# Five channels per selection matmul in the last group of a convolve-and-whiten kernel, and one load of the last pass moved

## The chip, the cores and the metric

The kernel runs on one core of a Trainium2 chip. The metric is the device time of one execution in microseconds (us). Engines are named as the profile names them: PE is TensorE (PEld its weight loads), DVE is VectorE, ACT is ScalarE, POOL is GpSimd, and SP is SyncE, which here issues most DMAs.

## The reference

The input x has 4 images of 64 channels of 256 x 256 pixels, f32. Layer 0 convolves every channel with its own 256 x 256 filter, which is the outer product of two filters of length 256 (each made by a small sine network), and adds `x * bias`. Layer 1 whitens the channels: the covariance of every ninth pixel, five Newton-Schulz steps towards its inverse square root, and that 64 x 64 matrix applied to all pixels.

```python
k = einsum('ijk,imk->ijmk', hx, hy)[0]            # separable filter of each channel
y = irfft2(rfft2(x, 512) * rfft2(k, 512) / 512)[..., :256, :256]
x = y + x * bias[:, None, None]
# layer 1
x1 = transpose(x, (1, 0, 2, 3)).reshape(64, -1)
x1_s = x1[:, ::9]                                  # every ninth pixel
mean1 = mean(x1_s, axis=-1, keepdims=True)
cov = x1_s @ x1_s.T / x1_s.shape[1] + 0.01 * eye(64)
out = newton_schulz_isqrt(cov, 5) @ (x1 - mean1)
```

## The kernel before

**First pass.** The work is cut into 32 steps `(g, n)`: a group g of 8 channels (`CG`) of image n. Step i holds its pixels in a buffer of `xpool`, which has four, so step i uses buffer i % 4. A step is done two channels at a time (c = 0, 2, 4, 6). `group` (L394) does the row convolution of two channels and the column convolution of the two channels of two positions earlier, as Toeplitz matmuls on PE. ACT copies the first result back, DVE adds `x * bias` to the second one in place (L412). Then `store` (L420) issues the two DMAs that write these channels to `y_d` in device memory, and `pack(2.92)` (L385) takes some operations from the list `todo`. The last two positions of the last step, (31, 4) and (31, 6), have no partner and go through `half_group(item, 1)` (L266), whose additions on DVE are those of L289; `pack(1.0)` follows each.

**Sampling.** Layer 1 needs every ninth pixel, and 256 is no multiple of 9, so each row of an image has its own phase. `pack_ops` (L313) gathers the samples of some channels into `samp[n]` with nine `copy_predicated` on DVE, one for each phase (L319); its source is every ninth element of a row. In the last two groups of channels a step hands over its first four channels as soon as they are stored, and its last four two positions later. `todo` takes the operations in order, each with a cost, and `pack` runs as many as its credit allows. The last four channels of the very last step, (7, 3), are packed by PE: `pack_by_pe` (L294) multiplies every ninth column of the pixels with `pick[:, s]`, a 128 x 128 selection matrix of phase s, and sums nine products in PSUM. It works on two channels at a time, for both halves b of the image's rows in one PSUM tile, and copies the result into `samp[3]` (L309, L311).

**Covariance and whitening.** `covariance(n)` (L327) multiplies the samples of an image, 58 matmuls (L333). After that of the last image a serial chain of small operations on PE, DVE and ACT (`whitening`, L460) makes the matrix W. `spin` (L437) issues matmuls whose result nobody reads. A matmul of f32 operands shows as two records of a weight load and two of a matmul in the profile.

**Last pass.** The 64 channels are read back from `y_d` in 32 pieces of 2 MB (`load_y`, L352), multiplied with W (L635), shifted by ACT and DVE (L639, L640) and stored (L645). Thirteen pieces have a home before any is stored: `homes` (L347) lists the pool of each, reusing buffers that the first pass has let go. The loads of pieces 0 to 8 are issued inside the first pass, at the places listed in `early` (L378), each behind the group of that place; pieces 9 to 12 come after the last matmuls of the first pass (L613). Piece 6 takes the buffer of step 29. Later loads wait until an earlier piece is stored.

**Order.** All instructions of the five engines of the first pass stand in the order in which the program writes them (`manual_schedule`); SP issues its DMAs in that order too.

The end of the first pass reads:

```python
for item in pending:              # (31, 4) and (31, 6)
    half_group(item, 1)
    pack(1.0)
    store(item)
pack()
...
for lo in range(CG // 2, CG, 2):
    pack_by_pe(g, n, yt, slice(lo, lo + 2))
spin(4)
covariance(NB - 1)
while len(loaded) < len(homes):
    load_next()
W, shift = whitening(i15, ones)
```

Of the kernel before, what the change touches and what calls it, by code (L numbers as in the profile page):

```python
# [38 lines left out]
F32 = mybir.dt.float32  # L39
# [7 lines left out]
P, H2 = 128, 2  # L47
EMB, ORDER = 33, 64
PIX = L * L
CG = 8  # L50
HP = P // 2
STEP = 9
NJ = 29
# [11 lines left out]
def conv_whiten_kernel(ctx: ExitStack, tc: tile.TileContext, a: dict, out: bass.AP):  # L65
    nc = tc.nc
# [9 lines left out]
    psA = ctx.enter_context(tc.tile_pool(name="psA", bufs=8, space=bass.MemoryType.PSUM))  # L76
# [23 lines left out]
    def load_x(t, g, n, c):  # L100
        nc.sync.dma_start(
            out=t[:, c : c + 2],
            in_=x[n, g][:, c : c + 2],
        )


    steps = [(g, n) for g in range(C // CG - 2) for n in range(NB)]
# [12 lines left out]
    samp = []  # L120
# [12 lines left out]
    def load_pick(lo, hi):  # L133
        for s in range(lo, hi):
            nc.scalar.activation(pick[:, s, :], ident, AF.Copy, scale=rows[:, s : s + 1])
# [47 lines left out]
    def new_toeplitz(g):  # L183


        return tpool.tile([P, 2, CG, L], F32, tag="toep", name=f"toep_{g}")

    def load_toeplitz(t, g, f, half, lo=0, hi=CG, issue=nc.sync):
        source, row = (g0_d, f * CG + lo) if g == 0 else (g_d, f * C + g * CG + lo)


        skip = 0 if f == half else HP
        issue.dma_start(
            out=t[half * HP : (half + 1) * HP, f, lo:hi, skip:],
            in_=bass.AP(
                tensor=source.tensor,
                offset=source.offset + row * GW + skip,
                ap=[[1, HP], [GW, hi - lo], [1, L - skip]],
            ),
        )  # L200
# [90 lines left out]
                        ALU.mult, ALU.add,  # L291
                    )

    def pack_by_pe(g, n, yt, cs):  # L294

        pk = psA.tile([P, H2, cs.stop - cs.start, NJ], F32, tag="psA", name=f"pk_{cs.start}")
        for s in range(STEP):
            for b in range(H2):
                nj = (L - s + STEP - 1) // STEP
                nc.tensor.matmul(  # L300
                    pk[:, b, :, 0:nj],
                    lhsT=pick[:, (s - b) % STEP, :],
                    rhs=yt[:, cs, b, s : s + STEP * (nj - 1) + 1 : STEP],
                    start=(s == 0 and b == 0),
                    stop=(s == STEP - 1 and b == H2 - 1),
                    skip_group_check=True,
                )
        dst = samp[n][:, :, :, g * CG + cs.start : g * CG + cs.stop]
        nc.scalar.copy(dst[:, 0], pk[:, 0].rearrange("p c j -> p j c"))  # L309
        copy = nc.vector.tensor_copy if cs.stop == CG else nc.scalar.copy  # L310
        copy(dst[:, 1], pk[:, 1].rearrange("p c j -> p j c"))  # L311

    def pack_ops(g, n, yt, cs):  # L313
        def op(s):
            nj = (L - s + STEP - 1) // STEP
            src = yt[:, cs, :, s : s + STEP * (nj - 1) + 1 : STEP].rearrange("p c b j -> p b j c")
            dst = samp[n][:, :, 0:nj, g * CG + cs.start : g * CG + cs.stop]
            m = mask[:, n, :, s : s + 1].unsqueeze(3).to_broadcast([P, H2, nj, cs.stop - cs.start])
            nc.vector.copy_predicated(dst, m, src)  # L319

        cost = 0.3 + 1.5e-3 * H2 * NJ * (cs.stop - cs.start)
        return [(cost, lambda s=s: op(s)) for s in range(STEP)]
# [4 lines left out]
    def covariance(n):  # L327

        pc = psA.tile([P, C + 1], F32, tag="psA", name=f"pc{n}")
        for b in range(H2):  # L330
            for j in range(NJ):
                half = slice(C * (j % 2), C * (j % 2 + 1))
                nc.tensor.matmul(  # L333
                    pc[half],
                    lhsT=samp[n][:, b, j, 0:C],
                    rhs=samp[n][:, b, j, :],
                    start=(b == 0 and j < 2),
                    stop=(b == H2 - 1 and j >= NJ - 2),
                    skip_group_check=True,
                )  # L340
        nc.vector.scalar_tensor_tensor(cov, pc, 1.0 / NSAMP, cov, ALU.mult, ALU.add)
# [18 lines left out]
    def load_next():  # L360
        loaded[len(loaded)] = load_y(len(loaded))

    loaded = {}
    todo = []
# [7 lines left out]
    for g in range(1, C // CG):  # L372
# [3 lines left out]
            blocks[k // 4, k % 4 * 2] = (g, part)  # L376

    early = {  # L378
        (26, 4): 1, (27, 0): 1, (27, 4): 1, (28, 0): 1, (29, 2): 1, (30, 0): 1, (31, 0): 1, (31, 2): 1, (31, 4): 1
    }  # L380
    orders = [list(range(L // HP)), list(reversed(range(L // HP)))]

# [2 lines left out]
    def pack(time=math.inf):  # L385
        credit[0] += time
        while todo and credit[0] > 0:
            cost, op = todo.pop(0)
            op()
            credit[0] -= cost  # L390
        if not todo:
            credit[0] = min(credit[0], 0.0)
# [27 lines left out]
    def store(second):  # L420
        g, n, c, yt, _ = second
        halves = g >= C // CG - 2
        for b in range(H2):
            row = b * C + g * CG + c
            nc.sync.dma_start(
                out=y_d[n][row : row + 2, :].rearrange("c (p w) -> p c w", w=L),
                in_=yt[:, c : c + 2, b],
            )

        if c == CG - 2 and (g, n) != steps[-1]:  # L430
            todo.extend(pack_ops(g, n, yt, slice(CG // 2 if halves else 0, CG)))
        elif c == CG // 2 - 2 and halves:
            todo.extend(pack_ops(g, n, yt, slice(0, CG // 2)))

    spins = []

    def spin(times):  # L437

        p = psA.tile([P, P], F32, tag="psA", name=f"spin{len(spins)}")
        spins.append(p)  # L440
        for _ in range(times):
            nc.tensor.matmul(p, lhsT=ident, rhs=ident, start=True, stop=True)  # L442
# [114 lines left out]
    with tc.manual_schedule(  # L557
        engines={engines.PE, engines.SP, engines.DVE, engines.Activation, engines.Pool}
    ):
        toep = {0: new_toeplitz(0)}  # L560

        for f, lo, hi in ((0, 0, 2), (0, 2, 4), (0, 4, 6), (1, 0, 2), (0, 6, 8), (1, 2, 4), (1, 4, 8)):
            for half in range(2):
                load_toeplitz(toep[0], 0, f, half, lo, hi, nc.scalar if half else nc.sync)
        for c in range(0, CG, 2):
            load_x(x_tiles[1], *steps[1], c)
        for i, (g, n) in enumerate(steps):
            xt = x_tiles[i % 4]
            for c in range(0, CG, 2):
                item = (g, n, c, xt, [])  # L570
                if g == C // CG - 1 and n > 0 and c == 2:
                    covariance(n - 1)
                if len(pending) == 2:
                    group(item, pending.pop(0))
                else:
                    half_group(item, 0)
                pending.append(item)
                if i == 0 and c == 6:

                    fold = const.tile([P, C], F32, tag="fold", name="fold")  # L580
                    nc.vector.tensor_tensor(fold, ident[:, 0:C], ident[:, C:P], ALU.add)

                    nc.scalar.activation(bf[:, 0:1], samp[0][:, 0, 0, C : C + 1], AF.Sqrt)
                if i == 1 and c < CG - 2:
                    load_pick(c // 2 * 3, c // 2 * 3 + 3)

                if i + 2 < len(steps):
                    load_x(x_tiles[(i + 2) % 4], *steps[i + 2], c)
                if (i, c) in blocks:
                    tg, part = blocks[i, c]  # L590
                    if part == 0:
                        toep[tg] = new_toeplitz(tg)
                    lo = part % 2 * CG // 2
                    load_toeplitz(toep[tg], tg, part // 4, part // 2 % 2, lo, lo + CG // 2)
                for _ in range(early.get((i, c), 0)):
                    load_next()
        g, n, c, yt, _ = pending[0]
        for item in pending:
# [5 lines that stand above are left out]
        i15 = place(2 * C, rows=C).rearrange("p (u c) -> p u c", u=2)  # L604
        for u in range(2):
            nc.gpsimd.tensor_scalar(i15[:, u], ident[0:C, 0:C], 1.5, None, ALU.mult)  # L606
        ones = place(P, rows=C)
        nc.gpsimd.memset(ones, 1.0)
        for lo in range(CG // 2, CG, 2):
            pack_by_pe(g, n, yt, slice(lo, lo + 2))  # L610
        spin(4)
        covariance(NB - 1)
        while len(loaded) < len(homes):  # L613
            load_next()
        W, shift = whitening(i15, ones)
# [3 lines left out]
    for i, (n, q) in enumerate(pieces):  # L619
        yt = loaded.pop(i)  # L620
# [5 lines left out]
        for w in range(FP // 1024):  # L626
# [6 lines left out]
            for k in range(2):  # L633
                for u in range(2):
                    nc.tensor.matmul(  # L635
                        po[u][halves[k]], lhsT=W[halves[u]], rhs=v[halves[u], k, cols],
                        start=True, stop=True,
# [68 lines left out]
```

## Time and profile before

| | |
|---|---|
| time, median of 3 runs | 903.08 us (902.95 to 903.26) |
| profiled execution | 903.93 us, of which the span from first to last instruction is 902.1 us |
| PE busy | 781.2 us, 87% of the span |
| DVE busy | 581.5 us, 64% |
| ACT busy | 395.5 us, 44% |
| DMA | 285.61 MB moved, 317 GB/s over the span |
| first pass: last Toeplitz matmul ends | about 619.4 us |
| covariance of the last image begins | 628.45 us |
| first matmul of the last pass | 643.18 us |

The profile is of one execution. A line of the timeline gives the start in us from the span's beginning, the duration, the engine, the source line, the operation, the tiles that it writes and reads, how many instructions were merged into the line, and in brackets the idle time before it and what ended it. A view by windows gives for stretches of time how long each engine was busy and, as the last two numbers, the mean busy share of the 16 DMA engines and the rate that they moved; such a share can come out a little above 1.

### The profile page before, as it was taken

The numbers are of one execution on the slowest core, as the hardware profiler recorded it, in microseconds if no ns is written. First come the engines' busy times: TensorE is split into PE (matmuls) and PEld (weight loads), VectorE is DVE, ScalarE is ACT, GpSimd is POOL, SyncE is SP. The second block draws the span as 40 slices with busy tenths as digits, with TensorE's granted clock in tenths as the row PEclk, the third lists the DMA queues.
The fourth block names the chain that finished last, engine by engine and source line by source line (L and its number), as shares of the span: only waits on it lengthen the run. The fifth ranks groups of instructions, "written<-read, shape, count | busy, mean of one in ns | idle before, by whom it ended". The sixth has DMA issues, their size and how long they took to land.

```text
span 902.1 us, 28046 instructions
## 1 busy us (share of the span) xinstructions
PE 781.2 (87%) x11928; PEld 647.5 (72%) x11928; DVE 581.5 (64%) x801; ACT 395.5 (44%) x676; POOL 14.5 (2%) x40
## 2 busy tenths in 40 slices
PE   8999999999999999999999999999999565666200
PEld 7999999999999999999999999999533111212000
DVE  3487778877888778877888877877688332233200
ACT  2655554545455555545454444442487232233200
POOL 1000000000000000000000000000010000000000
PEclk9999999999999999999999999999999766866755
DMA  7988889798788888888997899979999999999998
GB/s 209 327 262 252 242 261 271 234 273 251 247 263 261 244 264 259 258 250 267 293 275 241 285 351 356 335 237 390 375 401 429 430 432 432 429 434 430 430 430 355
DMA packets 117912, 285.61 MB, mean 317 GB/s; under 512 B 8891, under 2 KB 91116, under 8 KB 110108
## 3 DMA queue, kind: packets, MB, share of 16 engines
q1 hardware_dynamic: 113436, 244.94, 79.0%
q0 software_dynamic: 3056, 37.95, 10.0%
q8 instruction: 95, 1.56, 0.7%
q10 hardware_dynamic: 1296, 0.93, 0.4%
q14 instruction: 29, 0.24, 0.1%
HBM read 149.35 MB, written 134.44 MB: 315 GB/s over the span
## 4 chain that ended last, share of the span: by engine, by line
PE 74%; DMA 11%; another core or an unknown queue 7%; DVE 0%; issue 0%; SPq 0%; ACT 0%; POOLq 0%; DVEq 0%
PE p L220 64%; DMA out_dram<-yi 5%; DMA yi<-y_d 5%; PE po L635 4%; PE pc L333 2%; PE ph L252 1%; PE pk L300 1%; PE spin L442 1%; DMA toep<-g_d 0%; PE busy L152 0%; PE pm L158 0%; SPq L357 0%; DMA scratch<-in_zw_dram 0%; DVE yi L640 0%
## 5 line engine op out<-in xcount | busy, mean ns | idle before, releaser
L220 PE MATMUL p<-toep,x 64*64 64x64 f32 (+3 forms) x5040 | 579.5, 284 | 0.8 <-issue 0.8
L220 PE MATMUL p<-toep,o 64*64 64x64 f32 (+3 forms) x5040 | 579.5, 284 | 0.0
L220 PEld LDWEIGHTS p<-toep,x 64*128 64x128 f32 (+1 forms) x5040 | 535.7, 166 | 24.4 <-issue 1.3
L220 PEld LDWEIGHTS p<-toep,o 64*128 64x128 f32 (+1 forms) x5040 | 536.7, 166 | 10.7 <-issue 0.2
L409 ACT COPY o<-p 64x512 f32<-64x512 f32 x504 | 292.8, 581 | 294.2 <-PE p L220 286.6
L319 DVE COPY_PREDICATED samp<-mask,x 128x464 f32<-128x464 int32 (+3 forms) x351 | 297.2, 847 | 9.8 <-DVE x L412 0.2
L412 DVE SCALAR_TENSOR_TENSOR x<-x,bias,p 128x512 f32<-128x512 f32 x252 | 179.8, 744 | 121.3 <-PE p L220 117.3
L635 PE MATMUL po<-yi,chain 64*64 64x512 f32 x1024 | 143.7, 720 | 60.4 <-DMA yi<-y_d 60.4
L640 DVE TENSOR_SCALAR yi<-po,shift 128x512 f32<-128x512 f32 x128 | 96.1, 751 | 109.0 <-PE po L635 100.7
L635 PEld LDWEIGHTS po<-yi,chain 64*64 64x64 f32 x1024 | 48.0, 162 | 155.2 <-issue 150.5
L639 ACT ACTIVATE yi<-po,shift 128x512 f32<-128x512 f32 x128 | 88.0, 687 | 116.7 <-PE po L635 116.0
L333 PE MATMUL pc<-samp 128*64 128x65 f32 x464 | 14.9, 223 | 0.0
L333 PEld LDWEIGHTS pc<-samp 128*64 128x64 f32 x464 | 14.3, 137 | 0.3
L645 POOL DMA_DIRECT2D out_dram<-yi x19 | 10.5, 554 | 130.5 <-DMA out_dram<-yi 55.1
L606 POOL TENSOR_SCALAR chain<-ident 64x64 f32<-64x64 f32 x2 | 1.0, 519 | 606.6 <-PE ph L252 606.6
L286 DVE COPY o<-ph 64x256 f32<-64x256 f32 x8 | 3.4, 422 | 9.7 <-PE ph L252 9.6
L152 PE MATMUL busy<-idle 128*128 128x128 f32 x64 | 9.4, 307 | 0.0
L152 PEld LDWEIGHTS busy<-idle 128*128 128x128 f32 x64 | 8.9, 222 | 0.2 <-issue 0.2
L300 PE MATMUL pk<-x,pick 128*128 128x56 f32 (+1 forms) x72 | 8.3, 292 | 0.0
L300 PEld LDWEIGHTS pk<-x,pick 128*128 128x128 f32 x72 | 8.1, 192 | 0.1
L442 PE MATMUL spin<-ident 128*128 128x128 f32 x50 | 7.9, 292 | 0.0
L286 ACT COPY o<-ph 64x256 f32<-64x256 f32 x8 | 2.9, 368 | 10.7 <-DMA toep<-g_d 9.2
(93 smaller groups left out, 77.4 us busy)
## 6 DMA issues: line engine op xcount, KB each, us to landing
x<-in_x_dram SPq DMA_DIRECT2D x128, 512.0 KB, 5.3
y_d<-x SPq DMA_DIRECT2D x256, 256.0 KB, 3.5
yi<-y_d SPq DMA_DIRECT2D x32, 2048.0 KB, 15.6
out_dram<-yi POOLq DMA_DIRECT2D x17, 2048.0 KB, 67.7
out_dram<-yi SPq DMA_DIRECT2D x11, 2048.0 KB, 32.9
toep<-g_d SPq DMA_DIRECT2D x28, 256.0 KB, 6.3
toep<-g_d SPq DMA_DIRECT2D x29, 192.0 KB, 5.7
out_dram<-yi SPq DMA_DIRECT2D x4, 1024.0 KB, 32.8
```

The costliest lines, as they stand in the source:

```text
L152: nc.tensor.matmul(p, lhsT=idle[:, 0:P], rhs=idle[:, P : 2 * P], start=True, stop=True)
L220: mm = nc.tensor.matmul(ps[q : q + w, m, HP * k : L], lhsT=src[parts, k // 2, m * P + q : m * P + q + w], rhs=t[parts, : stop : -1] if k e ...
L300: nc.tensor.matmul(pk[:, b, :, 0:nj], lhsT=pick[:, (s - b) % STEP, :], rhs=yt[:, cs, b, s : s + STEP * (nj - 1) + 1 : STEP], start=(s == 0 ...
L319: nc.vector.copy_predicated(dst, m, src)
L333: nc.tensor.matmul(pc[half], lhsT=samp[n][:, b, j, 0:C], rhs=samp[n][:, b, j, :], start=(b == 0 and j < 2), stop=(b == H2 - 1 and j >= NJ ...
L409: nc.scalar.copy(o1[to], units[u][0][0][fr])
L412: nc.vector.scalar_tensor_tensor(x2[:, c2 + u], x2[:, c2 + u], bias[:, ch : ch + 1], units[u][1][0], ALU.mult, ALU.add,)
L442: nc.tensor.matmul(p, lhsT=ident, rhs=ident, start=True, stop=True)
L635: nc.tensor.matmul(po[u][halves[k]], lhsT=W[halves[u]], rhs=v[halves[u], k, cols], start=True, stop=True,)
L639: nc.scalar.activation(v[:, 0, cols], po[0], AF.Identity, bias=shift)
L640: nc.vector.tensor_scalar(v[:, 1, cols], po[1], shift, None, ALU.add)
L645: issue.dma_start(out=o[:, :, end - part : end], in_=v[:, :, end - part : end])
```

## The change

Three things change.

- Of the last step's eight channels DVE packs the first three instead of four (`LATE = 3`), so its nine `copy_predicated` there work on three channels each.
- `pack_by_pe` packs the other five in one go. There is one PSUM tile for each half b, and each selection matmul has five channels as its moving operand, 145 or 140 columns, where there were 58 or 56. So there are 18 matmuls where there were 36, and two copies of 145 elements a partition where there were four of 58: the first by ACT, the second by DVE. Five `spin` matmuls are put ahead of them.
- In `early` the load of piece 6 moves from (31, 0) to (30, 6), the position before it. SP issues it behind the group of that position, ahead of the two stores of (31, 0) that it followed before.

```diff
-    def pack_by_pe(g, n, yt, cs):
-        pk = psA.tile([P, H2, cs.stop - cs.start, NJ], F32, tag="psA", name=f"pk_{cs.start}")
-        for s in range(STEP):
-            for b in range(H2):
+    LATE = 3
+    def pack_by_pe(g, n, yt):
+        cs = slice(LATE, CG)
+        for b in range(H2):
+            pk = psA.tile([P, CG - LATE, NJ], F32, tag="psA", name=f"pk_{b}")
+            for s in range(STEP):
                 nj = (L - s + STEP - 1) // STEP
                 nc.tensor.matmul(
-                    pk[:, b, :, 0:nj],
+                    pk[:, :, 0:nj],
                     lhsT=pick[:, (s - b) % STEP, :],
                     rhs=yt[:, cs, b, s : s + STEP * (nj - 1) + 1 : STEP],
-                    start=(s == 0 and b == 0),
-                    stop=(s == STEP - 1 and b == H2 - 1),
+                    start=(s == 0),
+                    stop=(s == STEP - 1),
                     skip_group_check=True,
                 )
-        dst = samp[n][:, :, :, g * CG + cs.start : g * CG + cs.stop]
-        nc.scalar.copy(dst[:, 0], pk[:, 0].rearrange("p c j -> p j c"))
-        copy = nc.vector.tensor_copy if cs.stop == CG else nc.scalar.copy
-        copy(dst[:, 1], pk[:, 1].rearrange("p c j -> p j c"))
+            copy = nc.vector.tensor_copy if b else nc.scalar.copy
+            copy(samp[n][:, b, :, g * CG + LATE : (g + 1) * CG], pk.rearrange("p c j -> p j c"))
...
     early = {
-        (26, 4): 1, (27, 0): 1, (27, 4): 1, (28, 0): 1, (29, 2): 1, (30, 0): 1, (31, 0): 1, (31, 2): 1, (31, 4): 1
+        (26, 4): 1, (27, 0): 1, (27, 4): 1, (28, 0): 1, (29, 2): 1, (30, 0): 1, (30, 6): 1, (31, 2): 1, (31, 4): 1
     }
...
         elif c == CG // 2 - 2 and halves:
-            todo.extend(pack_ops(g, n, yt, slice(0, CG // 2)))
+            todo.extend(pack_ops(g, n, yt, slice(0, LATE if (g, n) == steps[-1] else CG // 2)))
...
-        for lo in range(CG // 2, CG, 2):
-            pack_by_pe(g, n, yt, slice(lo, lo + 2))
+        spin(5)
+        pack_by_pe(g, n, yt)
         spin(4)
         covariance(NB - 1)
```

## The prediction

> **What bounds the kernel.** I read the slices first (PE 0.9 busy up to 620 us, DMA at about 430 GB/s from 700 us on, so two stages with different limits), then the windows around the turn, with the DMA's share and rate as the last two numbers.
>
> ```profile
> 590.00:600.00 10.00, 10.00 (x235) 9.41 (x234) 8.88 (x16) 4.65 (x8) 0.00 (x0) 1.00 0.39 128
> 600.00:606.00 6.00, 6.00 (x88) 5.60 (x82) 2.81 (x6) 2.23 (x4) 0.00 (x0) 1.00 1.05 380
> 606.00:608.00 2.00, 2.00 (x32) 1.98 (x31) 1.65 (x3) 0.10 (x1) 0.00 (x0) 1.00 0.60 202
> 608.00:644.00 36.00, 34.83 (x460) 31.50 (x460) 22.16 (x59) 7.29 (x22) 1.15 (x3) 1.00 1.02 402
> 644.00:647.00 3.00, 3.00 (x32) 1.07 (x28) 2.31 (x4) 2.17 (x4) 0.00 (x0) 1.00 0.38 155
> 647.00:700.00 53.00, 52.67 (x493) 18.67 (x489) 45.86 (x62) 41.97 (x62) 6.79 (x12) 1.00 1.01 411
> 700.00:880.00 180.00, 87.17 (x504) 27.95 (x496) 47.97 (x64) 43.85 (x64) 3.74 (x7) 0.69 1.01 430
> ```
>
> From 608 us to the end the DMA is full, except at 644 to 647, where 0.62 x 3 = 1.86 us are lost: the 13 pieces that have a home have landed, and the first store is issued only at 645.57. After it, the remaining stores and loads run at the DMA's rate. So whatever delays the first store lengthens the kernel one for one; whatever hastens it gains at most these 1.86 us, about 0.2% (1.8 us), which is also about what a measurement of this kernel can tell from no change. What the first store waits for is the serial chain from the last Toeplitz matmul. The timeline of its PE part, then DVE's:
>
> ```profile
> 619.32 8.28 PE L300 MATMUL pk<-x,pick 128*128 128x58 f32 x72
> 627.42 1.10 PE L442 MATMUL spin<-ident 128*128 128x128 f32 x8
> 628.45 3.71 PE L333 MATMUL pc<-samp 128*64 128x65 f32 x116
> ```
> ```profile
> 618.59 1.30 DVE L319 COPY_PREDICATED samp<-mask,x 128x232 f32<-128x232 int32 x2
> 619.78 1.64 DVE L289 SCALAR_TENSOR_TENSOR x<-x,bias,ph 128x256 f32<-128x256 f32 x4
> 621.34 4.55 DVE L319 COPY_PREDICATED samp<-mask,x 128x232 f32<-128x232 int32 x7
> 627.89 0.22 DVE L311 COPY samp<-pk 128x58 f32<-128x58 f32 x1 [1.99 <-ACT samp L309]
> ```
>
> PE packs channels 4 and 5 while DVE's L289 still finishes 6 and 7 (to 621.42). The covariance (L333) starts 1.03 us after the spins do; the copies, done at 628.11, are hidden beneath them. Everything from L333 to the first store (645.57) is unchanged, so the question is when L333 starts.
>
> **When the new packing starts.** It needs channels 3 to 7, so the last L289. `copy_predicated` takes 627 ns for 232 elements and 1008 ns for 464 (the groups by form), 1.64 ns an element; three channels have 58 elements fewer, 0.095 us. Two of the nine lie ahead of that L289 (the order of the two kernels has the same two there): 621.42 - 0.19 = 621.23, and 0.06 us for the hand-over (L470 ends 633.06, its matmul's weights start 633.12): **621.3**, against 619.32. The five spins (10 records of 0.112 us, 1.1 us) fit into 619.4 to 621.3, where PE would wait: no cost. The other seven DVE operations end 0.85 us sooner, near 625.05, and matter only if PE is done by then.
>
> **What one record costs.** The 72 records of L300 come every 0.112 us (8.04 us from the first weight load to the first spin's), whether 58 or 56 columns: the load of 128 weight columns sets this pace, since the spins, with 128 columns, keep it too. With 16 records of 145 columns and 20 of 140 the moving operand takes over, and it is read with a step of nine elements. No such row is streaming bound, so I bound it:
>
> - *Below*: contiguous operands. 64x256 matmuls of L220 follow each other on one row tile every 0.214 us, 0.83 ns a column: 16 x 0.121 + 20 x 0.117 = **4.3 us** for the 36.
> - *Lag*: record by record, a matmul starts behind its own weight load by the streaming time of the matmul before: 54 ns after 64 contiguous columns, 107 to 110 after 128. In L300 it is 67 to 68 ns after 58 columns and 63 to 64 after 56, where contiguous ones would give 48 and 47. As a rate that is 1.15 ns a column: **5.9 us**.
> - *First of a group*: it starts with its weight load, so its duration shows its streaming.
>
> ```profile
> L300 PE MATMUL pk<-x,pick x72: 287/291/351, 619.3 to 627.3; 128*128 128x56 f32 x40, 128*128 128x58 f32 x32
> L457 PE MATMUL pw<-chain,chain x2: 272/296/321, 642.2 to 642.3; 64*128 64x65 f32 x2
> L442 PE MATMUL spin<-ident x50: 275/275/377, 627.4 to 643.0; 128*128 128x128 f32 x50
> ```
>
>   The maxima (third number) are these: 321 ns for 65 contiguous columns, 377 for 128, 0.89 ns a column; 351 for 58 strided ones is as many as 99 contiguous, 1.7 times the rate, 1.42 ns a column: **7.3 us**.
> - *Above*: two columns more lengthen the lag by 4 ns, 2 ns a column, as if a buffer hid a fixed part of a slower reading; 58 columns within 0.112 us cap it at 1.93 ns: **9.9 us**.
>
> I take twice the contiguous rate, 1.67 ns a column, between the last two: 16 x 0.242 + 20 x 0.233 = **8.5 us**. Twice the rate with 18 columns read ahead gives lags of (58 - 18) x 1.67 = 67 ns and (56 - 18) x 1.67 = 63 ns, both as read; a constant extra of 19 ns a record would give 66 for 56 columns, not 63. In the steady state a reader that is itself the limit gets no head start.
>
> [...]
>
> **The sum.** Weights to first spin: 621.3 + 8.5 = 629.8; the spin matmuls follow 0.06 later, L333 1.03 after them: 630.9, against 628.45. **2.5 us later.** The copies: 145 elements cost 226 ns + 87 x 1.06 ns (L412 744 ns for 512 elements, L289 473 for 256), 0.32 us. ACT's runs under the second tile's matmuls; DVE's starts some 0.35 us after the last matmul starts and ends before the spins do: nothing. If that cover went, it would cost 0.3. PSUM: four tiles instead of three reuse banks that L289 empties by 621.2: nothing.
>
> Pieces 11 and 12 wait on SP for L300 and for L333, so their loads go out 2.5 us later (12 at 632.24 now). The queue drains at 644.7, 12.5 us behind that, of which piece 12 needs 5 (2 MB at 415 GB/s): 7.5 us of slack hide it.
>
> **The moved load.** At (30, 6) SP reaches it after the stores near 593.5 and waits until DVE has packed step 29's last channels, at 595.08. Behind it on SP stand the stores of (31, 0), whose data are ready at 597.3: none is held up, and POOL's queue isn't touched. It moves 2 MB into 590 to 600, where the DMA is 0.39 busy. The queue ran nearly dry at 606 to 608 anyway (0.60), before piece 7 is issued at 607.16, so the loads behind it land no sooner: 0, at best the 0.8 us lost there, and that only if the chain hastens too; at worst the stores of (31, 0) land 3 us later, which nobody awaits.
>
> So the profiled execution's own 903.93 (span 902.1 and 1.8 around it) would become 906.4; it lies 0.85 above the median, and the same shift gives **905.6** for the median.
>
> **The rivals.**
> *The strided operand costs less than its lag suggests* (decided at 6.1 us for the 36 records, the break-even: 628.45 - 1.09 - 621.3). By the lag's rate of 1.15 ns L333 starts at 628.3, 0.2 sooner: 902.9, not slower. For: the lag is the plainest reading. Against: its slope of 2 ns a column, and the 351 ns.
> *Contiguous rate.* 4.3 us: packing ends 625.6, L333 starts 626.7, 1.75 sooner, nearly all of which the 1.86 us of DMA idle can give back: 901.3, faster, though hardly by more than can be told. For: the profile's ends of matmuls are modelled, so the 351 may be no streaming. Against: the lag, made of starts.
> *The moved load pays by itself*: the queue would have to be short of work nowhere from 600 us on; the 0.60 at 606 speaks against it. At most 0.8: 902.3.
>
> **Chances.** Double rate or worse (7.3 to 9.9 us, +1.2 to +3.8): 0.6, of which 0.52 lie above 904.9. Lag rate, 902.2 to 904: 0.25. Contiguous: 0.12, divided at 901.3. The load alone: 0.03. Faster by over 0.2% 0.11, within it 0.35, slower 0.54 (0.02 for a cost not seen). The range is from 902.0, leaving out the contiguous case, to 906.7.
>
> **What would show it.** Right: L300 with 36 records spread over 8 to 9 us, lags over 0.2 us, L333 near 630.9, the first store near 648.1, DMA idle of some 4.4 us between the loads' end and it, and DVE's packing done near 625 with nothing to do until L313's copy. Wrong: records every 0.12 us and L333 before 627; or pieces 11 and 12 landing after the chain ends, so that the idle does not grow.

## The result, and the profile after

The changed kernel takes 905.93 us (median of six executions, 905.5 to 907.36) against 902.92 us for the kernel before beside it (902.24 to 903.26): a ratio of 1.0036, with a 95% interval of 1.0025 to 1.0047. It is slower, by about 3 us, and 905.6 had been forecast. Its profiled execution took 905.69 us (span 903.9).

The last Toeplitz matmuls (L252) begin at 611.90 us here, in the profile before at 613.43; profiles of the runs below whose first pass is that of the changed kernel up to there have them anywhere from 611.90 to 613.71. So places below are counted from the first L252 matmul of the same profile. In the changed kernel L300 has become L304, L309 and L311 L313, L319 L321, L333 L335, L442 L444 and L645 L647; "before" in brackets is the kernel before.

The PE timeline of the changed kernel (start, duration, engine, line, operation, tiles, how many records, and in brackets the idle time before and what ended it):

```profile
611.90 5.96 PE L252 MATMUL ph<-toep,o 64*128 64x192 f32 x64
617.79 1.38 PE L444 MATMUL spin<-ident 128*128 128x128 f32 x10
619.34 9.45 PE L304 MATMUL pk<-x,pick 128*128 128x145 f32 x36 [0.17 <-DVE x L289]
628.61 1.07 PE L444 MATMUL spin<-ident 128*128 128x128 f32 x8
629.61 3.71 PE L335 MATMUL pc<-samp 128*64 128x65 f32 x116
```

Counted from L252, the packing begins at 7.44 (before: 5.89) and the covariance at 17.71 (before: 15.02), 2.69 us later. The 36 records fill the 9.27 us up to the spins, where the 72 of before filled 8.10. So 1.55 us of the 2.69 are the later start and 1.17 the longer packing; the spins take 0.03 less. DVE's timeline shows who waits for whom:

```profile
618.03 1.65 DVE L289 SCALAR_TENSOR_TENSOR x<-x,bias,ph 128x256 f32<-128x256 f32 x4
619.59 4.03 DVE L321 COPY_PREDICATED samp<-mask,x 128x174 f32<-128x174 int32 x7
628.83 0.31 DVE L313 COPY samp<-pk 128x145 f32<-128x145 f32 x1 [5.20 <-PE pk L304]
```

VectorE has packed its three channels by 623.62 and then stands idle for 5.2 us until TensorE has packed the other five. And the windows around the turn, of the changed kernel (last two numbers: the share of time that the 16 DMA engines were busy, and GB/s):

```profile
590.00:600.00 10.00, 10.00 (x249) 9.52 (x249) 7.79 (x14) 3.66 (x7) 0.00 (x0) 1.00 0.77 249
600.00:606.00 6.00, 6.00 (x67) 5.59 (x65) 3.70 (x6) 2.32 (x4) 0.00 (x0) 1.00 0.59 202
606.00:644.00 38.00, 36.52 (x429) 31.88 (x426) 21.46 (x60) 6.76 (x19) 0.94 (x3) 1.00 0.99 390
644.00:647.00 3.00, 3.00 (x28) 1.34 (x32) 1.14 (x3) 1.46 (x3) 0.00 (x0) 1.00 0.04 8
647.00:650.00 3.00, 3.00 (x32) 1.07 (x28) 2.71 (x5) 2.31 (x5) 0.00 (x0) 1.00 0.61 228
700.00:880.00 180.00, 87.46 (x512) 28.39 (x504) 48.56 (x65) 44.36 (x65) 3.73 (x7) 0.72 1.01 430
```

The last pass runs at the same 430 GB/s as before. At 644 to 650 the DMA lies idle for 2.88 + 1.17 = 4.05 us where the kernel before lost 1.86 (and at 643 to 644 its share is 0.12, before 0.92): the loads with a home have landed, and the first store is issued at 646.93, 35.03 us after L252 began (before: 32.14). The moved load shows too, as a share of 0.77 at 590 to 600 where it was 0.39, and of 0.59 at 600 to 606 where it was 1.05.

### The profile page after: what moved, and what is told of

The parts are those of the page before. It is cut to its first block, busy times and chain, and to the rows that moved or that the text cites. A ratio compares the mean times of both kernels' runs of the same rounds, so it can differ in the third digit from the quotient of the medians.

```text
span 903.9 us, 27995 instructions
## 1 busy us (share of the span) xinstructions
PE 781.8 (86%) x11902; PEld 647.4 (72%) x11902; DVE 580.3 (64%) x801; ACT 394.6 (44%) x674; POOL 14.3 (2%) x40
## 4 chain that ended last, share of the span: by engine, by line
PE 74%; DMA 12%; another core or an unknown queue 6%; DVE 1%; issue 1%; SPq 0%; ACT 0%; DVEq 0%; POOLq 0%
PE p L220 64%; DMA yi<-y_d 7%; DMA out_dram<-yi 5%; PE po L637 4%; PE pc L335 2%; PE pk L304 1%; PE ph L252 1%; PE spin L444 1%; PE busy L152 0%; DMA toep<-g_d 0%; PE pm L158 0%; DVE x L289 0%; SPq L359 0%; DMA scratch<-in_zw_dram 0%
## 5 line engine op out<-in xcount | busy, mean ns | idle before, releaser
L321 DVE COPY_PREDICATED samp<-mask,x 128x464 f32<-128x464 int32 (+5 forms) x351 | 296.4, 844 | 9.8 <-ACT o L411 0.2
L335 PE MATMUL pc<-samp 128*64 128x65 f32 x464 | 14.9, 223 | 0.0
L335 PEld LDWEIGHTS pc<-samp 128*64 128x64 f32 x464 | 14.3, 137 | 0.3
L647 POOL DMA_DIRECT2D out_dram<-yi x19 | 10.5, 552 | 133.8 <-DVE yi L642 58.2
L304 PE MATMUL pk<-x,pick 128*128 128x140 f32 (+1 forms) x36 | 9.4, 436 | 0.2 <-DVE x L289 0.2
L444 PE MATMUL spin<-ident 128*128 128x128 f32 x60 | 9.3, 291 | 0.0
L304 PEld LDWEIGHTS pk<-x,pick 128*128 128x128 f32 x36 | 7.4, 207 | 2.0 <-DVE x L289 0.4
L444 PEld LDWEIGHTS spin<-ident 128*128 128x128 f32 x60 | 7.6, 191 | 0.7
```

Of the source, the lines that this page charges most:

```text
L304: nc.tensor.matmul(pk[:, :, 0:nj], lhsT=pick[:, (s - b) % STEP, :], rhs=yt[:, cs, b, s : s + STEP * (nj - 1) + 1 : STEP], start=(s == 0), ...
L335: nc.tensor.matmul(pc[half], lhsT=samp[n][:, b, j, 0:C], rhs=samp[n][:, b, j, :], start=(b == 0 and j < 2), stop=(b == H2 - 1 and j >= NJ ...
L647: issue.dma_start(out=o[:, :, end - part : end], in_=v[:, :, end - part : end])
```

## The experiments

My theory: all of the loss is the packing, whose operand is read at every ninth element and so at half the contiguous rate (1.79 ns a column here, 0.83 in the prediction's contiguous matmuls), and whose delay goes one for one into the first store; the moved load is worth nothing. The rivals: the load shares in the loss or pays by itself; the later start or the idle DMA makes the loss, not the operand; and the delay is partly absorbed at the turn. Times of each run stand beside runs of the kernel before on the same chip.

### The packing alone

The changed kernel, with the entry in `early` put back:

```diff
-        (26, 4): 1, (27, 0): 1, (27, 4): 1, (28, 0): 1, (29, 2): 1, (30, 0): 1, (30, 6): 1, (31, 2): 1, (31, 4): 1
+        (26, 4): 1, (27, 0): 1, (27, 4): 1, (28, 0): 1, (29, 2): 1, (30, 0): 1, (31, 0): 1, (31, 2): 1, (31, 4): 1
```

> The changed kernel with the load of piece 6 back at (31, 0). Theory S: all of the 3.0 us comes from the packing (its matmuls stream a strided operand at 1.79 ns a column and start 1.5 us later), the load is worth nothing: 905.9 us, covariance of the last image 17.7 us after the first matmul of half_group (L252), as in the changed kernel. Rival L: the load's new place costs part of it (its 2 MB ahead of two stores): 904 to 905.

It took 906.28 us (five executions, 904.74 to 906.39), ratio 1.0035, interval 1.0023 to 1.0048: the whole loss, as the changed kernel. The covariance begins 17.72 after L252 in its profile (630.19 - 612.47).

### The load alone

The kernel before, with that entry alone changed:

```diff
-        (26, 4): 1, (27, 0): 1, (27, 4): 1, (28, 0): 1, (29, 2): 1, (30, 0): 1, (31, 0): 1, (31, 2): 1, (31, 4): 1
+        (26, 4): 1, (27, 0): 1, (27, 4): 1, (28, 0): 1, (29, 2): 1, (30, 0): 1, (30, 6): 1, (31, 2): 1, (31, 4): 1
```

> The kernel before with only the load of piece 6 moved to (30, 6). Theory S: 902.9 us, within 0.3 us of before, the DMA's idle time around 644 us as before (about 1.9 us) though the load goes out some 4 us sooner. Rival L: 904 us or more, or 902 if the load pays by itself.

It took 903.28 us (eleven executions) against 902.73 (twenty-one), ratio 1.0004, interval 0.9995 to 1.0013. The windows of this run:

```profile
590.00:600.00 10.00, 10.00 (x250) 9.50 (x248) 8.02 (x14) 3.94 (x7) 0.00 (x0) 1.00 0.72 248
600.00:606.00 6.00, 5.14 (x52) 4.96 (x50) 2.36 (x4) 2.32 (x4) 0.00 (x0) 1.00 0.38 128
606.00:644.00 38.00, 36.84 (x488) 33.41 (x488) 23.66 (x62) 7.27 (x22) 1.15 (x3) 1.00 1.01 399
644.00:647.00 3.00, 3.00 (x36) 1.07 (x32) 2.46 (x4) 2.31 (x4) 0.00 (x0) 1.00 0.31 119
```

The load runs sooner, and then the queue stands short of work sooner: 7.2 + 2.3 us of DMA time in the first 16 us, where the kernel before had 3.9 + 6.3. From 606 on nothing differs, and the covariance stays at 15.02 after L252.

### A contiguous operand

The changed kernel, with sizes, counts and waits as they are:

```diff
-                    rhs=yt[:, cs, b, s : s + STEP * (nj - 1) + 1 : STEP],
+                    rhs=yt[:, cs, b, s : s + nj],
```

> The changed kernel with the moving operand of each selection matmul contiguous within a channel (columns s to s + 28 instead of every ninth; the sampled pixels are other ones). Same 36 records of 145 or 140 columns, same place. Theory S: records every 0.12 us instead of 0.26, packing 4.4 us instead of 9.1, covariance about 13.2 us after the first matmul of L252 (before 15.0, changed 17.7), and of this only the 1.9 us of idle DMA before the first store can be won: 901.2 us. Rival W (the wait for the last L289 and the size of the tiles, not the step of the operand): records still every 0.25 us, 905.9 us.

It took 900.83 us (eleven executions), ratio 0.9981, interval 0.9973 to 0.999: faster than the kernel before. Its PE timeline:

```profile
619.14 4.60 PE L304 MATMUL pk<-x,pick 128*128 128x145 f32 x36
623.57 1.05 PE L444 MATMUL spin<-ident 128*128 128x128 f32 x8
624.56 3.71 PE L335 MATMUL pc<-samp 128*64 128x65 f32 x116
```

The same 36 records take 4.43 us to the spins instead of 9.27, about 0.12 us each, and the covariance begins 12.53 after L252. So without the step of nine elements there is no loss: the packing still begins later than in the kernel before (7.11 after L252, not 5.89), but its 3.67 us less outweigh that. The first store comes 29.86 after L252 (641.89), 2.28 sooner than before; of that 0.9981 is worth 1.7 us. It could not be worth more than the 1.86 us that the DMA lost before.

### The price by the step

The changed kernel, with every record at 145 columns:

```diff
-                nj = (L - s + STEP - 1) // STEP
+                nj = NJ
...
-                    rhs=yt[:, cs, b, s : s + STEP * (nj - 1) + 1 : STEP],
+                    rhs=yt[:, cs, b, 0 : (s + 1) * (nj - 1) + 1 : s + 1],
```

> The changed kernel with one thing altered: all 36 packing records move 145 columns (5 channels of 29), and the step between neighbouring columns is 1 element (4 bytes) for the first of the nine matmuls of a half, 2 for the second, and so on to 9 for the ninth (it reads other pixels than the reference). Read from the trace: the interval between record starts as a function of the step, in one look. Known ends: 0.120 us at step 1 (contiguous) and 0.260 us at step 9. [...] Theory B, the price grows with the distance: about 0.0175 us more for every step, 0.19 at step 5. Theory C, any step but 1 costs the whole: 0.26 from step 2 on.

One execution was taken, for its trace (906.05 us). Each step from 1 to 9 occurs as two records of 145 columns in each half. The differences between successive ends in the second half, from the trace, in us:

```
step (f32)    1     2     3     4     5     6     7     8     9
record      .126  .135  .194  .255  .269  .260  .262  .264  .261
record      .123  .137  .194  .258  .268  .262  .261  .263  .259
```

The price is neither one for any step (0.26 from step 2 on was theory C) nor proportional to it (theory B). A step of 2 costs 0.135 to 0.137 us, little more than the contiguous 0.123 to 0.126; a step of 3 costs 0.194, one of 4 0.255 to 0.258, and a wider one hardly more, 0.259 to 0.269 from 5 to 9. So nearly all of the price comes between steps 2 and 4, with step 3 as a stair between. At step 9 the 0.26 us are 1.79 ns a column, and the contiguous 0.123 to 0.126 are 0.85 to 0.87. Why the price ends at a step of four elements no run shows.

### A later start, not covered

The kernel before, with its two tiles in the other order:

```diff
-        for lo in range(CG // 2, CG, 2):
+        for lo in reversed(range(CG // 2, CG, 2)):
```

The condition for the copy by VectorE changes with it (`cs.stop < CG`), so that it is again the last tile's. Channels 6 and 7 come first, so the short records of before have to wait for L289.

> The kernel before with its two PE tiles in the other order (channels 6 and 7 first, then 4 and 5), so that packing starts only after the last L289, with 58-column records as before. Theory S: the records stay at 0.112 us, packing starts 2.1 us later and so does the covariance: 905.0 us; a late start alone costs its whole length. Rival W: the same or more, since the wait is all there is to it; if 903 or less, the start is hidden and the start term of my sum was wrong.

It took 912.63 us (four executions, 911.68 to 914.2), ratio 1.0113, interval 1.0098 to 1.0129: far above what I expected, by a cause that I had not in view. Its timeline, and windows with the granted clock (third number from the end):

```profile
619.69 13.90 PE L300 MATMUL pk<-x,pick 128*128 128x58 f32 x72 [1.68 <-DVE x L289]
```
```profile
619.70:621.90 2.20, 2.20 (x18) 2.11 (x19) 2.11 (x4) 0.00 (x0) 0.00 (x0) 1.00 1.06 373
621.90:639.00 17.10, 17.10 (x131) 16.88 (x132) 2.67 (x5) 0.56 (x3) 0.00 (x0) 0.50 0.96 384
639.00:641.00 2.00, 1.74 (x55) 1.60 (x51) 0.22 (x1) 0.00 (x0) 0.00 (x0) 0.99 0.53 221
```

TensorE does nothing for 1.68 us, and some 2 us after it works again the clock is halved, for 17 us: the same records start 0.213 us apart instead of 0.112, and the covariance 5.4 us instead of 3.71. The run says nothing on the delay itself. It shows, though, what the spins of the changed kernel stand in front of; so the next three take that apart.

### The later start with five spins, and with eight

The late start again, with `spin(5)`, and in a second run `spin(8)` in its place:

```diff
+        spin(5)
         for lo in reversed(range(CG // 2, CG, 2)):
```

> The kernel before with its two packing blocks in the other order (channels 6 and 7 first, 4 and 5 after them), as in the run before, but with five spin matmuls ahead of them that fill TensorE's wait for the last L289. Same 72 short records, begun about 2 us later. If a later covariance goes to the end one for one, as the prediction's sum had it: packing 2 us later, covariance 17.0 after the first L252 matmul instead of 15.0, time 902.9 + 2.0 = 904.9, 904.3 to 905.3, and the granted clock stays at 1. Rival, two us of delay are partly taken up by the transfers that wait at the turn: under 904.0.

With five: 904.83 us (ten executions), ratio 1.004, interval 1.0019 to 1.0062, but in two groups, seven at 903.58 to 905.39 and three at 910.56 to 911.7. The profiled execution is one of the three (910.89):

```profile
619.67 13.25 PE L300 MATMUL pk<-x,pick 128*128 128x58 f32 x72 [0.37 <-DVE x L289]
```
```profile
619.70:622.30 2.60, 2.60 (x22) 2.51 (x23) 2.50 (x5) 0.00 (x0) 0.00 (x0) 1.00 1.03 362
622.30:636.20 13.90, 13.90 (x89) 13.68 (x89) 2.25 (x5) 0.56 (x3) 0.00 (x0) 0.51 1.02 403
```

A gap of 0.37 us was left, and the clock fell here too; of the other nine executions no profile was taken. Hence the run with eight spins:

> The late start (the kernel before with channels 6 and 7 packed first) with eight spin matmuls instead of five, so that the gap of 0.37 us closes. With five, seven executions were at 903.6 to 905.4 and three at 910.6 to 911.7. Theory that the remaining gap lets the clock fall in some executions: all at 904.0 to 905.4, the clock at 1 throughout the packing, covariance 17.0 after the first L252 matmul. Rival, the short records (58 columns in 0.112 us) keep TensorE's clock at the edge by themselves and the gap is not what decides: again some executions at 910 to 912.

904.81 us (eleven executions, 904.03 to 906.54; before 902.85), ratio 1.0023, interval 1.0014 to 1.0032; none near 910. No gap stands before the packing, and the clock stays at full:

```profile
617.70 2.05 PE L442 MATMUL spin<-ident 128*128 128x128 f32 x16
619.58 8.31 PE L300 MATMUL pk<-x,pick 128*128 128x58 f32 x72
628.74 3.71 PE L333 MATMUL pc<-samp 128*64 128x65 f32 x116
```
```profile
619.70:627.00 7.30, 7.30 (x67) 7.24 (x66) 4.32 (x8) 0.33 (x2) 0.00 (x0) 1.00 1.07 407
```

This is the clean test of the delay: the covariance begins 16.93 after L252 instead of 15.02, 1.91 later, and the time is 1.96 us longer. One for one, and nothing is taken up at the turn.

### The changed kernel without its five spins

```diff
-        spin(5)
         pack_by_pe(g, n, yt)
```

> The changed kernel without the five spin matmuls ahead of its packing: TensorE then does nothing for about 1.4 us between the last L252 matmul and the first packing record. I costed these spins at nothing because they lie in a wait. Theory that their cover matters: the granted clock falls as it did in the run with the packing begun late (0.5 to 0.65 for some 20 us after a gap of 1.7 us), records and covariance take about half as long again, and the time goes to 911 to 916. Rival, that gap is too short to lower the clock: the packing begins at the same point and the time stays at 905.9, 905.3 to 906.5.

906.39 us (five executions, 905.65 to 906.55), ratio 1.0038, interval 1.0025 to 1.005: as with the spins. But not because the clock held:

```profile
620.12 9.45 PE L304 MATMUL pk<-x,pick 128*128 128x145 f32 x36 [1.49 <-DVE x L289]
```
```profile
621.90:625.20 3.30, 3.30 (x15) 3.25 (x14) 2.36 (x5) 0.20 (x1) 0.00 (x0) 0.51 1.16 419
625.20:629.40 4.20, 4.20 (x19) 3.46 (x18) 0.00 (x0) 0.09 (x1) 0.00 (x0) 0.98 0.92 375
```

It fell to half for 3.3 us, and the packing still took its 9.45 us: the strided records came every 0.26 us at half the clock too. The covariance began 17.71 after L252 (630.39 - 612.68), exactly as with the spins. So both theories were half right: the clock is halved after the gap, and here that costs nothing.

### Three channels instead of five

The changed kernel with another `LATE`; the second run has `spin(8)` for its `spin(5)` too:

```diff
-    LATE = 3
+    LATE = 5
```

> The changed kernel with LATE at 5: TensorE packs three channels with each selection matrix (87 and 84 columns instead of 145 and 140), VectorE five. At 1.79 ns a column the 36 records take 0.156 and 0.150 us each, 5.5 us in all instead of 9.3; the covariance then begins 17.7 - 3.8 = 13.9 to 14.3 us after the last group's first L252 matmul, where the kernel before had 15.02. VectorE's packing of five channels needs 0.7 us more than that of three and ends near 625, beside TensorE's. Theory that covariance start goes to the end one for one: 902.9 - 0.8 = 902.1 us, 901.7 to 902.6. Rival, the price is one for each record and not for each column (0.26 us again): 905.9, as the changed kernel.

With five spins: 903.21 us (eleven executions, 901.99 to 905.72; before 902.78), ratio 1.0011, interval 1.0002 to 1.0021, and above the 902.1 expected. Its profiled execution was the fastest:

```profile
619.41 5.82 PE L304 MATMUL pk<-x,pick 128*128 128x87 f32 x36 [0.56 <-DVE x L289]
626.05 3.71 PE L335 MATMUL pc<-samp 128*64 128x65 f32 x116
```

5.64 us from the first record to the spins, 0.157 a record where the five channels took 9.27 / 36 = 0.258: the price is one for each column, not for each record. The covariance begins 14.47 after L252 (626.05 - 611.58), 0.55 sooner than before, where 13.9 to 14.3 had been expected: the packing begins 7.83 after L252 and not 7.44, since VectorE's two operations ahead of the last L289 now take five channels. Four of the eleven executions lay at 904.69 to 905.72, and a gap of 0.56 us stands ahead of the packing; in this execution the clock stayed at 1.00 behind it. With eight spins:

> The three-channel version with eight spin matmuls ahead of the packing instead of five, so that TensorE's gap of 0.56 us before the packing closes to under 0.3 us. The three-channel version had two groups of times: seven executions at 902.0 to 903.3 and four at 904.7 to 905.7. Theory that the gap sometimes lets the clock fall (as in the profile of the late start with five spins, where the gap was 0.37 us): with the gap closed only the lower group stays, median 902.3, 901.7 to 903.3, none over 904. Rival, the upper group has another cause: a third of the executions still at 904.7 to 905.7 and the median near 903.2.

902.63 us (eleven executions, 901.65 to 903.29; before 902.85), ratio 0.9997, interval 0.9988 to 1.0006. The upper group is gone. That its cause was the clock is likely from the late starts above, but no execution of that group was profiled, and four of eleven against none of eleven is a thin count, as is three of ten against none of eleven with the late start. The covariance begins at 14.46 and the first store 31.78 after L252, 0.36 us sooner than before, which is too little to tell. So no version that takes every ninth pixel beat the kernel before.

## Why the prediction was right

*What sets the end.* Right. A covariance 2.69 us later gave a first store 2.89 us later and a time 3.01 us longer; 1.91 gave 1.96 with the short records; and in the other direction 2.28 us gave 1.7, as the idle DMA allows. The chain from the covariance to the first store, put down as unchanged, took 17.32 us instead of 17.12; it did so in every profile with the new packing (17.32 to 17.35), and why is open.

*When the packing starts.* The step that put it at 621.3, behind the last L289, failed by 0.43 us. VectorE had its four L289 done 7.78 after L252, as forecast (621.23 is 7.80). But the first record begins 0.05 us after the third of the four ends, 0.34 us ahead of the fourth's end. I had overlooked that the first tile reads only half 0 of the image's rows, which by the code the first two additions write. In the contiguous run, and in the run by the step, whose first record is contiguous, it does begin 0.05 us after the second; why the strided one waits for the third is open. The start came at 7.44, where 7.87 was forecast.

*What one record costs.* That the strided operand would set the pace was right, and the size 7% low: 1.79 ns a column, not 1.67; 9.02 us from first weight load to the first spin's, not 8.5. Of the three readings of the profile the closest was one that I used only as the upper end: the lag's growth of 4 ns for two columns, 2 ns a column; the 1.67, twice the contiguous rate, was a choice between two of them, where the run by the step gives 1.79 against 0.85 to 0.87, some 2.1 times. The first of a group gave 1.42 because it took the rest of such a record's duration from contiguous ones; two strided records show the rate without that. It lasts 351 ns with 58 columns and 506 with 145, so 155 / 87 = 1.78 ns, which leaves 248 ns for the rest, where 0.89 ns a column leaves some 263 to the contiguous ones. The lag as a rate and the contiguous rate, the two rivals, were far off; what the second would have been worth the contiguous run shows: 4.43 us, and a gain capped by the idle DMA.

*From packing to covariance.* The term of 0.06 us by which the spins' matmuls follow their weights came out as 0.25, because the first spin stands behind a slow record. These 0.19 more, +0.52 for the packing, -0.43 for the start and -0.03 for the spins (1.00 us, not 1.03) make up the 0.24 us between 2.45 and 2.69 but for rounding. That the total came out within 0.3 us is in part luck: the kernel before took 0.16 us less beside it than when the forecast was made, and without the error in the start the others would have put the covariance 0.67 us off.

*The hidden parts.* VectorE's idle wait, forecast from 625.05 (11.62 after L252), began at 11.72. Copies, PSUM and pieces 11 and 12 cost nothing that shows. The moved load at nothing agrees with its own run, 1.0004 (0.9995 to 1.0013).

*The spins at nothing.* The number was right, the reason incomplete. I priced what they take, not what they prevent. Without them the granted clock is halved for 3.41 us and the time stays, because these records take their 0.26 us at half the clock too. Ahead of the short records a like gap costs 912.63 - 904.81 = 7.8 us. With the window set on the stretch at half clock, the three profiles (without the spins, the late start, the late start with five) read:

```profile
621.97:625.38 3.41, 3.41 (x15) 3.37 (x14) 2.29 (x5) 0.29 (x1) 0.00 (x0) 0.50 1.19 428
621.96:639.03 17.07, 17.07 (x131) 16.84 (x131) 2.62 (x5) 0.56 (x3) 0.00 (x0) 0.50 0.96 386
622.64:636.29 13.65, 13.65 (x87) 13.43 (x88) 1.95 (x4) 0.56 (x3) 0.00 (x0) 0.50 1.01 401
```

They are one, five and four times 3.41 us; why, no run shows. The length of the gap alone does not decide: gaps of 1.49 and 1.68 us, and in one profiled execution one of 0.37, were followed by half the clock here, while one of 0.56 ahead of the three channels was followed by no fall.

*The idle DMA* grew, as forecast: 4.05 us in the two windows and 0.88 more at 643 to 644, against some 4.4. The loads ran out sooner in that execution, whose first pass was 1.5 us ahead.

## What to carry to other kernels

Before matmuls are merged into longer ones, see what sets their pace. Here records with 128 weight columns came every 0.112 us whether their moving operand had 56 or 58 strided columns or 128 contiguous ones, so that 58 strided columns came free; with 145 each column cost 1.79 ns at a step of nine elements. A step of two f32 elements was nearly free (0.136 us against 0.124 for 145 columns), and one of four (0.257) about as dear as any up to nine (0.259 to 0.269). Hand over to TensorE only as many columns as end together with VectorE's share, and look at who then idles; here that brought the time back to the kernel before (0.9997), not below it. And where a stall moves ahead of short records, fill it to the last few tenths of a microsecond (0.37 us was left in an execution of 910.89): several executions, not one profile, show whether that was enough.

## What the runs showed that I had not expected

- A gap in TensorE's work of 1.5 to 1.7 us was followed, some 2 us after work had begun again, by half the clock (0.50 granted): for 3.41 us with long strided records, for 17.07 us with short ones, whole multiples of 3.41. Why it stayed low longer with the short records is open. In the kernel before they ran for 8.10 us at a granted clock of 1.00, so there they did not lower it by themselves.
- With five spins ahead of the late start, seven executions took about 904.5 us and three about 911. A cost of 6 us that comes only sometimes can be missed by a single execution.
- Records of 145 strided columns hold their 0.26 us at half the clock, while those of 58 go from 0.112 to 0.213.
